# Output projection of an attention layer as seven block products over the whole sum, with its rows turned by DMA, in a kernel on one core

## The chip, the cores and the metric

The kernel runs on one core of a Trainium2 chip. A core has five engines that work side by side, each with its own queue of instructions: TensorE (PE; its weight loads are listed as PEld), VectorE (DVE), ScalarE (ACT), GpSimd (POOL) and SyncE (SP), from whose queue most transfers (DMA) are issued. The metric is the device time of one execution in microseconds, as a median over runs.

## The reference, cut to what matters

An input x of 8 batches, 512 rows, 256 columns goes through four blocks, each added to x after a layer normalization: a linear attention with normalized keys and queries, a feed-forward block (here "f"), a softmax attention with 16 heads of 64, and the same feed-forward block again (here "g").

```python
concat = ctx.reshape(ctx.shape[0], ctx.shape[1], H * P)   # 16 heads x 64 = 1024
out = concat @ l_w.T + l_b                                # 1024 -> 256
...
x = x + _L0_attn_b_ref(_layernorm(x, axis=-1), ...)
x = x + _L0_ffn_ref(_layernorm(x, axis=-1), ...)
```

The change concerns `concat @ l_w.T + l_b`, of 512 x 1024 by 1024 x 256 in each batch. All data are float32; a matmul on float32 shows as two instructions in the profile.

## The kernel before, in words

**Stages.** The heads are worked in pairs, 8 pairs per batch and 64 in all. A loop takes two pairs at a time (32 rounds). In a round, `attend` issues a fixed sequence of score matmuls (line 1081), the maximum (DVE, 1086), exponents (ACT, 1097) and context matmuls (1134); it lasts 13.8 us on PE. It leaves a 128x512 context tile (`ctx`, pool `cpool`) for each pair. Between two such sequences lies a stretch in which PE does everything else: the front of a coming batch (normalizations, linear attention, feed-forward f), projections of queries and keys for the next two pairs (`project_pairs`), of values (`values_fast`), the output projection (`project_out`, label `y`), and the tail of an earlier batch (normalization, feed-forward g, storing).

**Products in blocks.** `project_pairs`, `values_fast` and `keys` already use a scheme of seven block products in place of eight (`seven`): sums of weight blocks are made once, differences of row blocks on POOL for each batch (lines 825 and 573), and seven products are added up in PSUM and by ACT and DVE as they leave it (lines 869, 879, 889, 925, 933). The output projection does not: `project_out` computes rows of x by `rows` (line 429), half of the pairs at a time, with the context as the loaded weights and the output weights `al` as moving data; DVE adds each result from PSUM into x (line 1017).

**Turning rows.** A normalized tile must be transposed. `normed_t` does this on PE; `normed_dma` splits the float32 values into 16-bit parts on POOL (line 408), turns them by a DMA transpose on SP's queue (413), and joins the parts on POOL (417).

**Order.** The order of the instructions on each engine is worked out when the program is built. Every piece of work is a generator that yields its next step: engine, estimated time, time at which its inputs are ready. `Order` keeps an own clock for each engine and picks the step that can start first; among those that start within 0.4 us the one with the lowest rank. A piece has a due period (a pair number) by which it must be done, and a lead, by which its rank falls below that. `until` runs what is due, `fill` adds what fits in a share of PE time. `CHOICES` has for each round a change of the share, a slack and a number that perturbs the ranks. Engines take their instructions in the order so written; real waits go by semaphores. `take` picks one of five PSUM places for a product.

**Buffers.** `buffers(True)` is a set of tiles `xn`, `xr`, `xk`, used by the front of batch 1 and then by the tails of batches 0 to 6; `buffers(False)` serves the other fronts and batch 7's tail. The output bias `lb` is added to x on POOL after each front (line 770).

## Time and profile before

| | us |
|---|---|
| median of 3 runs | 1145.85 (1145.68 to 1146.25) |
| span of the profiled execution, first to last instruction | 1144.2 |
| PE busy | 1124.5 |
| DVE busy | 795.8 |
| ACT busy | 675.1 |
| POOL busy | 461.2 |
| output projection on PE, 512 instructions, summed latencies | 116.1 |

The profile comes from one execution; its own time is given by its span, and the medians of the runs lie 1.65 us above that. Busy times are sums over the instructions of an engine. A matmul's listed time is its latency; matmuls overlap, so that the distance between two starts is what one costs. "PE idle" is time in which no matmul is under way.

### The profile page before, as it was taken

To read this page: it belongs to the slowest core of one execution; us is meant where nothing else is said; L and a number is where in the kernel's file an instruction comes from. 1 tells how busy PE (TensorE), PEld (TensorE's weight loads), DVE (VectorE), ACT (ScalarE), POOL (GpSimd) and SP (SyncE) were. 2 spreads that over 40 slices of the span, in tenths; PEclk is the share of its full clock that TensorE was granted. 3 is DMA by queue.
4 is the path that set the end of the run, shared out by engine and by line. 5 is a ranking of instruction groups with operands and counts; after the bars stand their busy time and mean duration, and the time that the engine had idled before them with its cause. 6 is when DMAs were issued, how large, how long until landed. Compare 5 with 4: busy or idle time off the path is not lost.

```text
span 1144.2 us, 19158 instructions
## 1 busy us (share of the span) xinstructions
PE 1124.5 (98%) x7006; PEld 701.7 (61%) x7006; DVE 795.8 (70%) x1444; ACT 675.1 (59%) x1777; POOL 461.2 (40%) x736
## 2 busy tenths in 40 slices
PE   7999999999999999999999999999999999999998
PEld 4655466655656666666567657666565666666556
DVE  5776767776777676777856767677776776766664
ACT  3546765476564664657645675457765467454653
POOL 4456333352432363344732546353362534421311
PEclk9999999999999999999999999999999999999999
DMA  8000000010001010011010211101101010000001
GB/s 298 1 1 1 10 10 10 11 28 11 1 11 46 19 20 19 1 46 29 19 19 1 56 20 19 19 20 46 19 11 28 19 20 19 10 19 2 19 1 38
DMA packets 61181, 28.63 MB, mean 25 GB/s; under 512 B 51456, under 2 KB 59648, under 8 KB 60576
## 3 DMA queue, kind: packets, MB, share of 16 engines
q1 hardware_dynamic: 59936, 25.70, 9.3%
q8 instruction: 56, 0.92, 0.3%
q10 hardware_dynamic: 864, 1.05, 0.3%
q0 software_dynamic: 288, 0.67, 0.2%
q14 instruction: 37, 0.30, 0.1%
HBM read 10.63 MB, written 4.19 MB: 13 GB/s over the span
## 4 chain that ended last, share of the span: by engine, by line
PE 49%; DVE 1%; POOL 1%; issue 1%; ACT 0%; POOLq 0%; DVEq 0%
PE cx L1134 10%; PE sc L1081 10%; PE m_qk L917 9%; PE y L429 6%; PE m_v L953 4%; PE kv L661 2%; PE r_g L429 2%; PE o_g L429 1%; PE m_k_g L580 1%; PE r_f L429 1%; PE o_f L429 1%; PE k_f L540 1%; PE q L429 1%; DVE xkFalse L733 0%; PE k_g L540 0%
## 5 line engine op out<-in xcount | busy, mean ns | idle before, releaser
L1097 ACT ACTIVATE e<-sc,nm 128x512 f32<-128x512 f32 x512 | 346.7, 689 | 130.0 <-DVE nm L1086 129.8
L1086 DVE TENSOR_REDUCE nm<-sc 128x2 f32<-128x1024 f32 x256 | 308.7, 1218 | 72.1 <-PE sc L1081 71.3
L1081 PE MATMUL sc<-qk 64*64 64x512 f32 x2048 | 263.8, 593 | 3.1 <-DVE qk L889 3.0
L1134 PE MATMUL cx<-e,vs 64*64 64x512 f32 x2048 | 262.3, 589 | 1.0 <-DVE v L974 0.6
L1114 POOL TENSOR_TENSOR vs<-v,rs 128x256 f32<-128x256 f32 x128 | 78.8, 616 | 376.2 <-DVE rs L1110 368.2
L1134 PEld LDWEIGHTS cx<-e,vs 64*64 64x64 f32 x2048 | 85.0, 133 | 136.9 <-issue 114.7
L1081 PEld LDWEIGHTS sc<-qk 64*64 64x64 f32 x2048 | 74.4, 132 | 137.7 <-issue 87.4
L429 PE MATMUL y<-al,ctx 128*128 128x256 f32 x512 | 116.1, 380 | 0.0
L429 PEld LDWEIGHTS y<-al,ctx 128*128 128x128 f32 x512 | 96.7, 190 | 16.3 <-ACT e L1097 2.4
L1097 ACT ACTIVATION_READ_ACCUMULATOR e<-sc,nm 128x1 f32 x512 | 105.4, 206 | 0.0
L925 ACT ACTIVATE qk<-m_qk,bias 128x256 f32<-128x256 f32 x124 | 52.1, 475 | 76.2 <-PE m_qk L917 76.0
L1142 DVE TENSOR_TENSOR ctx<-cx,ctx 128x512 f32<-128x512 f32 x64 | 44.3, 691 | 47.3 <-ACT ctx L1141 47.3
L933 DVE SCALAR_TENSOR_TENSOR qk<-m_qk,dbias,qk 128x256 f32<-128x256 f32 x124 | 54.2, 479 | 20.1 <-PE m_qk L917 19.3
L1017 DVE TENSOR_TENSOR x<-y,x 128x512 f32<-128x512 f32 x32 | 22.1, 689 | 47.7 <-PE y L429 47.7
L661 PE MATMUL kv<-wkv,xrFalse 128*128 128x512 f32 x112 | 52.5, 605 | 0.2 <-DVE st_n L357 0.2
L417 POOL COPY xrFalse<-xkFalse 128x1024 uint16<-128x1024 uint16 x22 | 29.1, 1336 | 44.1 <-DMA xkFalse<-xrFalse 44.1
L1141 ACT COPY ctx<-cx 128x512 f32<-128x512 f32 x64 | 37.4, 584 | 10.8 <-PE cx L1134 10.8
L408 POOL COPY xrFalse<-xnFalse 128x512 uint16<-128x512 uint16 x68 | 39.4, 611 | 6.6 <-ACT xnFalse L381 6.6
L917 PE MATMUL m_qk<-xta,aq 128*128 128x256 f32 x124 | 38.7, 393 | 0.0
L607 POOL TENSOR_TENSOR x<-x,xkFalse 128x512 f32<-128x512 f32 x24 | 30.7, 1283 | 18.0 <-DVE xkFalse L558 7.9
L917 PE MATMUL m_qk<-xta,sums_q 128*128 128x256 f32 x124 | 37.8, 387 | 0.1
L917 PE MATMUL m_qk<-xts,aq 128*128 128x256 f32 x124 | 37.6, 385 | 0.0
(259 smaller groups left out, 1908.6 us busy)
## 6 DMA issues: line engine op xcount, KB each, us to landing
out<-x SPq DMA_DIRECT2D x16, 256.0 KB, 2.1
x<-in_x SPq DMA_DIRECT2D x6, 512.0 KB, 4.3
aq<-in_aq SPq DMA_DIRECT2D x1, 1024.0 KB, 7.8
ak<-in_ak SPq DMA_DIRECT2D x1, 1024.0 KB, 9.9
av<-in_av SPq DMA_DIRECT2D x1, 1024.0 KB, 11.9
al<-in_al SPq DMA_DIRECT2D x1, 1024.0 KB, 14.3
xkFalse<-xrFalse SPq DMA_TRANSPOSE x34, 3.1
x<-in_x ACTq DMA_DIRECT2D x4, 128.0 KB, 4.0
```

The source lines that it names most:

```text
L429: nc.tensor.matmul(ps[:, u * D : (u + 1) * D], lhsT=lhs[i][:, u * P : (u + 1) * P], rhs=rhs[i], start=(i == 0), stop=(i == n - 1),)
L661: nc.tensor.matmul(ps, lhsT=xt[:, kc, u * P : (u + 1) * P], rhs=wkv[:, kc, :], start=(kc == 0), stop=(kc == KC - 1),)
L917: nc.tensor.matmul(ps[:, w * HS : (w + 1) * HS], lhsT=lhs[w][n - 1], rhs=block_of_rows(b, n), start=start and w == 0, stop=True, skip_grou ...
L925: nc.scalar.activation(dst[:, w, :], ps[:, w, :], AF.Identity, bias=bias[:, w, p : p + 1])
L933: nc.vector.scalar_tensor_tensor(dst[:, w, :], ps[:, w, :], dbias[:, w, p // 2 : p // 2 + 1], part[:, w, :], ALU.add, ALU.add,)
L953: nc.tensor.matmul(ps[:, u * HS : (u + 1) * HS], lhsT=block_of_rows(b, n)[:, u * P : (u + 1) * P], rhs=rhs[n - 1], start=start and u == 0, ...
L1081: nc.tensor.matmul(ps[m * HD : (m + 1) * HD, j, :], lhsT=kt[hs, keys], rhs=qt[hs, :], start=True, stop=True,)
L1086: nc.vector.tensor_reduce(nm, ps, AX.X, ALU.max, negate=True)
L1097: nc.scalar.activation(e[:, j, :], ps[:, j, :], AF.Exp, bias=nm[:, j : j + 1], accum_out=sums[g, h][:, c % 2, j : j + 1],)
L1114: nc.gpsimd.tensor_tensor(vs, vh[b, p // 4][:, 2 * h : 2 * h + 2, cols].rearrange("p t (j d) -> p t j d", j=2), rs.unsqueeze(3).to_broadca ...
L1134: nc.tensor.matmul(cx[m][j * HD : (j + 1) * HD, :], lhsT=vsc[g, c // 2][ks, c % 2, j, :], rhs=es[g, c][ks, j, :], start=(c == 0), stop=(c ...
L1142: nc.vector.tensor_tensor(ct, cx[1], ct, ALU.add)
```

## The change: what it does

For batches 0 to 6 the output projection is written in the scheme of seven products. The output is split in two halves of columns and two halves of rows, the sum of 1024 in even and odd pairs (four groups of two pairs). Each product adds all four groups in PSUM, so that it covers the whole sum. The weights `al` are now the loaded operand and the context the moving one, so the result comes out transposed. Sums of weights are made once on POOL (`sums_of_output`), one of them in place of a quarter of `al`, which is loaded again at batch 6. `differences` makes twelve differences of context blocks on POOL, `last_differences` four more. The bias `lc` enters as the results leave PSUM on ACT, the difference of its halves, `dlc`, on DVE. `rows_of_output` turns the result back by two POOL copies, a DMA transpose and a POOL cast per half, and DVE adds it into x. Batch 7 keeps the old form and the old addition of `lb`.

`project_out_fast` of a batch is added in the round of the first two pairs of the next batch (`p == 1`), due in that same period; before, the two halves of the pairs were due at two different periods. It works in `buffers(True)` and waits for the tail of the batch before.

Besides: due periods and leads come from a table, the front is split in three pieces with their own due periods, `CHOICES` is new, some entries moving single pieces in rank, `take` prefers the lowest place and not the highest, three pools have other numbers of buffers, batch 2's first normalization is turned by DMA, and the last batch's second normalization takes the form with two POOL operations and the scaling on DVE. (`CHOICES` and the small helpers `copy`, `add` and `shifted`, which are one instruction each, are left out below.)

```diff
+PLAN = {
+    "linear 0": (-1, 8), "linear 1": (-3, 8), "linear": (-9, 8),
+    "queries 0": (-1, 8), "queries 1": (-3, 8), "queries": (-9, 8),
+    "mean 0": (-1, 8), "mean 1": (-3, 8), "mean": (-9, 8),
+    "front 0": (-1, 8), "front 1": (-3, 8), "front": (-3, 8),
+    "ffn 0": (-1, 8), "ffn 1": (-3, 8), "ffn": (-3, 8),
+    "norm 0": (-1, 8), "norm 1": (-3, 8), "norm": (-3, 8),
+    "rows": (-1, 8), "tail": (15, 0), "keys": (15, 0), "tail last": (17, 16), "tail 6": (17, 0), "keys 6": (17, 0), "pairs": (0, 8),
+    "values 1": (2, 8), "values 0": (4, 8), "y": (0, 8), "y differences": (0, 8),
+    "y rows": (4, 8), "y plain": (2, 0), "y last": (11, 16), "scale": (0, 128),
+    "v 0": (-1, 0), "v 1": (3, 0), "project": (-1, 0), "sums": (0, 0), "late sums": (5, 0),
+}
...
-    def __init__(self, gen, due, lead, number):
-        self.gen, self.due, self.rank, self.number = gen, due, due - lead, number
+    def __init__(self, gen, kind, at, number):
+        due, lead = PLAN[kind]
+        self.gen, self.kind, self.base, self.number = gen, kind, at, number
+        self.due = at + due
+        self.rank = self.due - lead
         self.advance(None)
...
-        a = [(max(t, at), -i) for i, t in enumerate(self.banks) if unheld(t)]
+        a = [(max(t, at), i) for i, t in enumerate(self.banks) if unheld(t)]
...
-    small = ctx.enter_context(tc.tile_pool(name="small", bufs=8))
-    epool = ctx.enter_context(tc.tile_pool(name="epool", bufs=6))
-    cpool = ctx.enter_context(tc.tile_pool(name="cpool", bufs=8))
+    small = ctx.enter_context(tc.tile_pool(name="small", bufs=7))
+    epool = ctx.enter_context(tc.tile_pool(name="epool", bufs=5))
+    cpool = ctx.enter_context(tc.tile_pool(name="cpool", bufs=9))
...
+        nc.gpsimd.dma_start(out=lc, in_=a["lb"].rearrange("(k p) -> p k", p=P))
...
-        ps, ready = yield from normed_t(xb, name, s, h, ready, early=name in ("f0", "f1"))
+        ps, ready = yield from normed_t(xb, name, s, h, ready, early=name in ("f0", "f1", f"g{B - 1}"))
...
-        if b < 3:
+        if b < 2:
...
-        yield "G", 1.3, ready
-        xh = xb[:, 2 * h : 2 * h + 2, :]
-        nc.gpsimd.tensor_tensor(xh, xh, lb.to_broadcast([P, 2, D]), ALU.add)
+        if b == B - 1:
+            yield "G", 1.3, ready
+            xh = xb[:, 2 * h : 2 * h + 2, :]
+            nc.gpsimd.tensor_tensor(xh, xh, lb.to_broadcast([P, 2, D]), ALU.add)
...
+    def output_blocks():
+
+        s = blocks["sums_y"]
+        v = al.rearrange("p (g i) d -> p g i d", i=2)
+        a11, a21, a12, a22 = (v[:, :, i, j * P : (j + 1) * P] for i in range(2) for j in range(2))
+        s1, s2, s4 = (s[:, i, :].rearrange("p (g c) -> p g c", c=P) for i in range(3))
+        return a11, a12, s4, a22, s1, s2, a21
+
+    def sums_of_output():
+
+        a11, a12, s4, a22, s1, s2, a21 = output_blocks()
+        for dst, x0, x1, op in (
+            (s1, a21, a22, ALU.add), (s2, s1, a11, ALU.subtract), (s4, a12, s2, ALU.subtract),
+            (a21, a11, a21, ALU.subtract),
+        ):
+            ready = yield "G", 1.3, 0.0
+            nc.gpsimd.tensor_tensor(dst, x0, x1, op)
+        order.marks["sums_y"] = ready
+
+    def differences(b, ready):
+
+        yield "G", 0.0, ready, -1, ("y", b, "room")
+        s = buffers(True)
+        t3, t2 = (s[n].rearrange("p h (g s) -> p (h g) s", g=2) for n in ("xr", "xk"))
+        for i in range(3):
+            for g in range(NP // 2):
+                (b11, b12), (b21, b22) = halves_of_context(b, g)
+                ready = yield "G", 0.6, ready
+                dst, x0, x1 = (
+                    (t3[:, g, :], b22, b12), (b12, b12, b11), (t2[:, g, :], b22, b12),
+                )[i]
+                nc.gpsimd.tensor_tensor(dst, x0, x1, ALU.subtract)
+            order.marks["y", b, i] = ready
+
+    def last_differences(b, ready):
+
+        t2 = buffers(True)["xk"].rearrange("p h (g s) -> p (h g) s", g=2)
+        for g in range(NP // 2):
+            b21 = halves_of_context(b, g)[1][0]
+            ready = yield "G", 0.6, ready
+            nc.gpsimd.tensor_tensor(b21, b21, t2[:, g, :], ALU.subtract)
+        order.marks["y", b, 3] = ready
+
+    def halves_of_context(b, g):
+
+        return [[ctxt[b, 2 * g + i][:, j * HS : (j + 1) * HS] for j in range(2)] for i in range(2)]
+
+    def project_out_fast(b):
+
+        for h in range(2):
+            if b:
+                yield "G", 0.0, 0.0, -1, ("g", b - 1, h)
+        order.marks["y", b, "room"] = 0.0
+        order.add(differences(b, 0.0), "y differences", NP * b + 9)
+        s = buffers(True)
+        lhs = output_blocks()
+        t3, t2 = (s[n].rearrange("p h (g s) -> p (h g) s", g=2) for n in ("xr", "xk"))
+        rhs = []
+        for g in range(NP // 2):
+            (b11, b12), (b21, b22) = halves_of_context(b, g)
+            rhs.append([b11, b21, b22, b21, b12, t2[:, g, :], t3[:, g, :]])
+        c = [[chunks(s["xn"], j)[:, i, :] for j in range(2)] for i in range(2)]
+
+        def product(n, mark, ps=None):
+            ready = yield "T", 2 * FAST, 0.0, -1, mark, ps is None
+            i = None
+            if ps is None:
+                i = order.take()
+                ps = psum_tile(i, f"m{n}_y_{b}")
+                ps = (ps[:, 0, :] if i < PAIRS else ps)[:, :HS]
+                first = True
+            else:
+                first = False
+            for g in range(NP // 2):
+                nc.tensor.matmul(
+                    ps, lhsT=lhs[n - 1][:, g, :], rhs=rhs[g][n - 1],
+                    start=first and g == 0, stop=True, skip_group_check=True,
+                )
+            return i, ps, ready
+
...
+        i1, ps1, p1 = yield from product(1, "sums_y")
+        u1 = yield from copy(c[0][0], ps1, p1)
+        i6, ps6, p6 = yield from product(6, ("y", b, 2))
+        u2 = yield from add(c[1][0], ps6, c[0][0], max(u1, p6))
+        order.give(i6)
+        i7, ps7, p7 = yield from product(7, ("y", b, 0))
+        u3 = yield from shifted(c[1][1], ps7, c[1][0], max(u2, p7))
+        _, _, p2 = yield from product(2, None, ps1)
+        order.add(last_differences(b, p2), "y differences", NP * b + 9)
+        c11 = yield from copy(c[0][0], ps1, max(p2, u2))
+        order.give(i1)
+        i5, ps5, p5 = yield from product(5, ("y", b, 1))
+        c22 = yield from add(c[1][1], ps5, c[1][1], max(p5, u3))
+        _, _, p3 = yield from product(3, None, ps5)
+        c12 = yield from add(c[0][1], ps5, c[1][0], max(p3, u2))
+        order.give(i5)
+        order.add(rows_of_output(b, 1, max(c12, c22)), "y rows", NP * b + 9)
+        _, _, p4 = yield from product(4, ("y", b, 3), ps7)
+        c21 = yield from shifted(c[1][0], ps7, c[1][0], max(p4, c12))
+        order.give(i7)
+        if b == B - 2:
+            nc.sync.dma_start(
+                out=al.rearrange("p (g i) d -> p g i d", i=2)[:, :, 0, P:],
+                in_=a["al"].rearrange("p (g i) d -> p g i d", i=2)[:, :, 0, P:],
+            )
+        order.add(rows_of_output(b, 0, max(c11, c21)), "y rows", NP * b + 9)
+
+    def rows_of_output(b, h, ready):
+
+        s = buffers(True)
+        apart, turned, y = (s[n].bitcast(U16)[:, h, :] for n in ("xr", "xk", "xn"))
+        columns = y.rearrange("p (k r) -> p k r", k=KC)
+        for k in range(KC):
+            ready = yield "G", 0.6, ready
+            nc.gpsimd.tensor_copy(
+                apart.rearrange("p (l u k d) -> p l u k d", l=2, k=KC, u=2)[:, :, :, k, :],
+                columns[:, k, :].rearrange("p (u d l) -> p l u d", l=2, u=2),
+            )
+        ready = yield "S", 0.9, ready
+        nc.sync.dma_start_transpose(
+            out=turned.rearrange("p (g r) -> p g r", r=P), in_=apart
+        )
+        ready = yield "G", 1.25, ready
+        nc.gpsimd.tensor_copy(
+            y.rearrange("p (u d l) -> p l u d", l=2, u=2),
+            turned.rearrange("p (l u d) -> p l u d", l=2, u=2),
+        )
+        ready = yield "V", 0.62, ready
+        xt = half_of(x[b], h)
+        nc.vector.tensor_tensor(xt, s["xn"][:, h, :], xt, ALU.add)
+        order.add(tail(b, h, ready), "tail 6" if b == B - 2 else "tail", NP * b)
+
...
+    order.add(sums_of_output(), "late sums")
...
+    total -= 7 * 2 * FAST
...
-        if p == 5:
-            order.add(project_out(b, 0), g + 2)
+        if p == 5 and b == B - 1:
+            order.add(project_out(b, 0), "y plain", g)
+        if p == 1 and b > 0:
+            order.add(project_out_fast(b - 1), "y", g)
```

## The prediction

> **What bounds the kernel now.** I read the head of the profile page first, then its chain of waits, then TensorE's (PE's) own waits, then the rows of the operations that the change touches, then the stretches in which the new work must fit.
>
> ```profile
> span 1144.2 us, 19158 instructions
> PE 1124.5 (98%) x7006; PEld 701.7 (61%) x7006; DVE 795.8 (70%) x1444; ACT 675.1 (59%) x1777; POOL 461.2 (40%) x736
> ...
> PE 49%; DVE 1%; POOL 1%; issue 1%; ACT 0%; POOLq 0%; DVEq 0%
> ```
>
> PE is busy 98% of the span, and the chain that ended last is nearly all PE (the shares sum to about half of the span because some matmul records are missing). The next engine stands at 70%. Twenty microseconds are without a matmul, and the stretches say where:
>
> ```profile
> 0.00:30.00 30.00, 22.50 (x74) 13.36 (x74) 16.35 (x47) 12.23 (x39) 14.36 (x35) 1.00 0.79 285
> ...
> 900.00:1050.00 150.00, 149.97 (x993) 95.07 (x995) 107.48 (x182) 84.34 (x216) 52.25 (x78) 1.00 0.07 17
> ...
> 1140.00:1144.20 4.20, 0.00 (x0) 0.00 (x0) 1.10 (x2) 0.00 (x0) 0.00 (x0) 0.97 0.18 62
> ```
>
> The columns are length, then busy time of PE, weight load, DVE, ACT and POOL, then the granted clock. The head loses 7.5 us and the last 4.2 us have no matmul; in the middle PE idles 0.03 us in 150. Adding the loss at each of 32 changes between the 64-wide and the 128-wide matmuls (rows of 8 and 4 that take 1.02 and 1.06 us where the same take 0.86) gives 0.36 x 32 = 11.5 us, which stays whatever the order. So time goes away one for one with PE work, and an order alone has perhaps 5 us to win in the middle.
>
> **What the skill says.** "SBUF — State Buffer", section "Who interferes with whom": a DVE instruction with two SBUF inputs contends with a POOL instruction that reads SBUF, and the second one to issue waits. The trace agrees: the DVE operation of line 733 has a median of 478 ns and a longest of 1493. "PSUM — Partial Sum Buffer", section "Engine vs sequencer instructions": ACT, DVE and POOL queues are strict FIFO, and matmuls start in program order. No matmul in this trace starts ahead of an earlier one, so a product that waits for POOL holds back all PE work behind it. "GPSIMD Engine Reference", section "Elementwise — side-by-side cycle accounting", has POOL about twice as slow as DVE for two inputs; the trace has 1.27 us against 0.69 us for 128x512.
>
> **The change part by part.** These rows carry the prices:
>
> ```profile
> L429 PE MATMUL y<-al,ctx 128*128 128x256 f32 x512 | 116.1, 380 | 0.0
> L1017 DVE TENSOR_TENSOR x<-y,x 128x512 f32<-128x512 f32 x32 | 22.1, 689 | 47.7 <-PE y L429 47.7
> L825 POOL TENSOR_TENSOR xts<-xta x16: 722/727/1252, 93.8 to 979.0; 128x256 f32<-128x256 f32 x16
> L408 POOL COPY xrFalse<-xnFalse 128x512 uint16<-128x512 uint16 x68 | 39.4, 611 | 6.6 <-ACT xnFalse L381 6.6
> L417 POOL COPY xrTrue<-xkTrue 128x1024 uint16<-128x1024 uint16 x14 | 18.5, 1336 | 5.8 <-DMA xkTrue<-xrTrue 5.8
> L770 POOL TENSOR_TENSOR x<-x,lb 128x512 f32<-128x512 f32 x16 | 20.2, 1270 | 1.2 <-ACT xnFalse L381 1.2
> xkTrue<-xrTrue SPq DMA_TRANSPOSE x14, 3.1
> ```
>
> A matmul's row shows its latency (380 ns), not its cost: the chain has "y L429 x16" in 3.45 us, 0.2157 us each from start to start.
>
> 1. *PE, products.* A batch's output projection is 512/8 = 64 instructions, 13.80 us. The new form has seven products of four pair sums in two passes, 7 x 4 x 2 = 56 instructions of the same 128x128 by 256 form, 12.08 us. Weight loads keep their 190 ns below 216 ns and stay hidden. Seven batches: 7 x 8 x 0.2157 = **12.08 us less** on the path.
>
> 2. *PE, transposes.* Batch 2's first normalization goes over to the DMA transpose: 8 PE transposes of 0.109 us (four take 0.43 in the timeline), **0.87 us less**. In return: four POOL copies and two casts (4 x 0.61 + 2 x 1.34 = 5.1 us) and two DMA transposes of 3.1 us; two ACT copies go (1.2 us). POOL is 48% busy between 60 and 150 us, and the new due time is 6 pair steps ahead of need, so I cost it at nothing; uncovered it is one latency of some 8 us, once.
>
> 3. *POOL.* Gone: 14 of 16 bias additions, 14 x 1.27 = 17.8 us. Added per batch: 12 + 4 differences of 128x256, 16 x 0.727 = 11.6 us, and for two halves two copies and a cast each, 2 x (2 x 0.61 + 1.34) = 5.1 us; seven batches 117 us. Once: four sums of weights, 4 x 1.27 = 5.1 us. Batch 2's 5.1 as above. POOL goes from 461 to about 571 us, half the span: hidden as a total. It is not hidden where a product waits for it (below).
>
> 4. *DVE and ACT.* Gone: 28 additions x 0.69 = 19.3 us. Added per batch: three additions of 0.42 and two shifted joins of 0.48 from PSUM, and two additions of 0.69 into x, 3.6 us, 25 in all. DVE gains 6 us of 796, ACT two copies of 0.475 per batch, 6.7 us of 675. Both have 30% or more free: nothing.
>
> 5. *SP's queue.* 16 more transposes. They stand among output stores and other transposes and each holds SP until its copies are done. SP already waits 325.8 us ahead of output stores with no harm to PE. The reload of a quarter of the weights (256 KB) at batch 6 also waits on SP, for the last product. The nearest loads, 256 KB, land in 3 to 6 us, and the plain products of batch 7 come two periods (some 60 us) later: nothing. A late load would cost those few microseconds, once.
>
> 6. *Small.* One more short bias load from POOL's queue at about 21 us (0.55 us of POOL) in the head, 0 to 0.6 us. The shift it feeds sits beside the DVE step at 63.6 us, 35 us after landing at the neighbours' 6 us. One fewer exponent buffer: in the second half of an attention step the exponents then wait for the context matmuls issued just ahead of them. Those end 0.86 us after the scores; the maximum that the exponents wait for anyway takes 1.22 us. Covered by 0.36 us; the tenth context tile is likewise needed only after the products, which are due before it. The last batch's earlier normalization has two POOL operations fewer (0.22 + 0.20) and DVE in place of ACT (2 x 0.41 against 1.1 us): 0.5 us gained at an end where PE has gaps of 0.36 and 0.16 us; I take 0.3.
>
> 7. *The new order and its waits.* A product waits for twelve differences: 12 x 0.727 = 8.7 us, while the planner counts 0.6 each, 7.2 us. They can start about 1.7 us into the stretch between two attention steps, after the two scalings of values that end there (511.49 and 512.60 in the timeline, 509.84 being the stretch's start). So product six is ready about 10.5 us in. Ahead of it can go product one (1.73 us), the seven steps of the next pair (28 x 0.2157 = 6.04 us), and the value products (6.04 us): 13.8 us, enough by 3.3. Behind product six wait all other PE work and then the attention step. If the planner puts product six just at its own ready time, PE loses 1.5 us in that batch. The last product waits four differences, 2.9 us, under two products of 1.73: covered. A product added into a bank that DVE has just read waits 0.42 + about 0.2 us if nothing lies between. From zero to about 2.1 us a batch, 0 to 15 in all; the work at hand speaks for the lower part. I take 0.25 us x 7 = 1.75 us. A new order may also win back up to about 3 of the 5 us; I count none.
>
> The sum on the profile's span: 1144.2 - 12.08 - 0.87 - 0.3 + 1.75 = 1132.7 us. The median stands 1.65 us above the span, so **1134.3 us**.
>
> **Rivals.** (a) *Partial stalls.* Product six and the last product come late by 0.7 to 1.5 us in most batches, as the planner's 0.6 us suggests; 5 to 10 us return, 1137.5 to 1142.5. For it:
>
> ```profile
> 747.74:771.21 23.47, 23.41 (x103) 18.37 (x105) 17.79 (x36) 11.50 (x32) 15.47 (x25) 1.00 0.07 23
> 886.10:909.44 23.34, 23.31 (x98) 17.68 (x100) 16.35 (x36) 10.05 (x31) 12.50 (x20) 1.00 0.04 12
> ```
>
> These are two of the seven stretches in which the new products stand. POOL is busy 12.5 and 15.5 of 23.4 us already; 11.6 more makes 24 to 27. Against it: the due times move other POOL work away, and fourteen bias additions go. (b) *POOL becomes the bound of these stretches, slower than before.* The differences queue behind 5 to 6 us of other POOL work, and PE stands at product six. The change is even at 13.25 - 7k = 0, k = 1.9 us per batch, and slower by 0.2% from 2.2 us. With k = 3 us (product six ready near 14 us, 11 us of work ahead of it), 21 us return: 1145.85 - 13.25 + 21 = 1153.6 us. Against it: PE is in-order but its order is written with POOL's load counted. (c) *The order wins too.* PE's middle losses shrink by 3 us or more: 1129.5 us and below. (d) *The gain is hidden*, because PE was not the limit: within 0.2% of 1145.85. The 149.97 of 150 us speaks against it.
>
> **How the numbers follow.** Covered, 1131 to 1137: 0.58, and the forecast is 1134.3. (a) 0.24, of which 0.02 lies within 0.2%. (b) 0.08. (c) 0.08. (d) 0.02. 0.2% (2.3 us) is about what a measurement can tell from no change. Faster 0.58 + 0.22 + 0.08 = 0.88, same 0.04, slower 0.08. The range takes in the covered case, (a) nearly whole, and the nearer part of (c): 1129 to 1142 us. The likeliest case's own range is 1131 to 1137.
>
> **What would show it.** After: the y matmuls fall to 7 x 56 + 64 = 456; PE busy falls by about 13 us to near 1111; POOL near 570. A wait row of PE or its weight loads on POOL for the y products shows step 7, and its total says which case holds: below 3 us covered, 5 to 10 (a), over 15 (b). DVE rows of two SBUF inputs grow in mean if the shared port bites. The forecast is wrong if the stretches after the first attention step of each batch show PE idle by more than 1 us, if the attention steps grow longer than 13.8 us for want of buffers, or if the end after the last context matmul, 28.8 us now, grows because batch 6's tail comes late (at most about 5 us).

## The result, and the profile after

| | before | after |
|---|---|---|
| median, us | 1146.04 (11 runs, 1145.68 to 1147.15) | 1143.57 (11 runs, 1142.37 to 1144.73) |
| span of the profiled execution, us | 1144.2 | 1142.3 |

The ratio is 0.9976, with a 95% interval of 0.9967 to 0.9985. The change makes the kernel about 2.5 us faster. The forecast was 11.6 us, and 1143.57 lies outside its range, 1129 to 1142. One execution of a later kernel (new products with the old settings) took 2452 us, its 256-wide matmuls 0.443 us apart where 0.216 is usual; no ratio below uses it.

The head of the page after, and the shares of the chain of waits:

```profile
span 1142.3 us, 19417 instructions
PE 1116.8 (98%) x6942; PEld 698.6 (61%) x6942; DVE 805.7 (71%) x1470; ACT 676.4 (59%) x1785; POOL 568.8 (50%) x883
...
PE 88%; DVE 6%; ACT 3%; issue 1%; POOL 1%; DMA 1%; DVEq 0%; POOLq 0%; ACTq 0%
```

PE has 64 matmuls fewer, as worked out (7 x 8 of products and 8 of transposes). Its busy time falls by only 7.7 us. A matmul's listed time is its latency, and of the time that is lost below about half lies under a listed matmul. POOL is at the 571 us of the prediction. The chain's shares can't be set beside those of before as they stand: the chain before is followed back only to 547.6 us, so its shares cover half of the span (missing matmul records, which the prediction gave as the reason, were not shown to be it). From about 548 us to the end, some 595 us in both, DVE holds 13.8 us of the chain before and 26.6 after, ACT 2.3 and 12.2. So time that passes through these two engines has come onto the path.

The same stretches as before, columns as in the prediction:

```profile
0.00:30.00 30.00, 22.52 (x71) 12.56 (x71) 15.18 (x45) 12.09 (x39) 14.07 (x35) 1.00 0.80 284
...
450.00:600.00 150.00, 147.74 (x925) 94.81 (x928) 108.28 (x193) 88.82 (x237) 81.32 (x126) 1.00 0.14 27
...
900.00:1050.00 150.00, 149.29 (x981) 95.48 (x983) 101.68 (x173) 83.63 (x215) 71.55 (x105) 1.00 0.12 24
```

The head is unchanged. In the middle PE is without a matmul for 0.71 us of the 150 from 900 us on, where it was 0.03. Over the five such windows from 300 to 1050 us it is 7.4 us (150 less each PE time, 147.74 the lowest), and was 1.6 before.

Groups of instructions that the change added, and one (line 753) that it did not touch:

```profile
L1129 PE MATMUL m_y<-ctx,al 128*128 128x256 f32 x168 | 39.7, 379 | 0.0
...
L753 DVE SCALAR_TENSOR_TENSOR xkFalse<-xkFalse,rnq,gf 128x256 f32<-128x256 f32 x28 | 23.3, 876 | 3.4 <-ACT gf L741 3.3
...
L1095 POOL TENSOR_TENSOR ctx<-ctx,xkTrue 128x256 f32<-128x256 f32 x28 | 19.5, 728 | 8.0 <-PE m_y L1129 8.0
```

The last number of the first row says that PE was never idle ahead of these products, and the three other forms of the new products have the same 0.0. So the wait that steps 7, (a) and (b) of the prediction turned on does not exist. The second row is a scaling in a batch's front that is the same instruction as before. There it had a mean of 704 ns (line 733); now it has 876.

Two waits of PE are new. These rows give the wait, its total in us, how often it came and its longest; the kernel before has neither:

```profile
PE m_qk L949 <- DVE qk L965: 4.5, 7, 0.7
PE sc L1258 <- ACT e L1274: 3.8, 6, 1.1
```

**Where the 12.95 us of PE work went.** The distances between the starts of consecutive matmuls, summed once over the attention steps (64-wide matmuls) and once over the stretches between them, close the account. Work is the number of matmuls times the undisturbed distance of their form; what is left of a stretch is idle.

| us | before | after | change |
|---|---|---|---|
| ahead of the first matmul | 6.55 | 6.34 | -0.2 |
| PE work in the stretches | 658.41 | 645.46 | -12.95 |
| idle in the stretches | 25.9 | 30.0 | +4.1 |
| attention steps | 448.59 | 455.28 | +6.7 |
| after the last matmul | 4.8 | 5.2 | +0.4 |

The saving is there to the hundredth (12.08 + 0.87). 10.8 us of it is given back in two places, neither of which is a wait of the new products.

**First place: the attention steps.** A step takes 13.9 us in both kernels as a rule. Before, four steps took longer, by 2.6 us together. After the change twelve do, by 9.7 us: the five behind the fourth stretches by 6.8, one other by 1.2 (13.9 us when the changed kernel was run again), and six behind third stretches by 1.7. In nearly every batch the stretches between the steps follow one pattern, from batch 1 on with 24.2, 16.4, 7.8 and 31.0 us of PE work. The steps behind the fourth stretch take 15.14, 15.65, 14.95, 15.65 and 14.95 us, the one other 15.10, and the steps behind the third stretch 14.1 to 14.3. This is the timeline at the start of such a step, all engines, many lines left out (start, duration, then engine and line; PE's scores begin at 456.17):

```profile
454.89 1.26 POOL L627 TENSOR_TENSOR x<-x,xrTrue 128x512 f32<-128x512 f32 x1 [0.37 <-DVE xrTrue L578]
455.01 1.81 DVE L753 SCALAR_TENSOR_TENSOR xkFalse<-xkFalse,rnq,gf 128x256 f32<-128x256 f32 x2 [0.20 <-ACT gf L741]
456.17 1.09 PE L1258 MATMUL sc<-qk 64*64 64x512 f32 x8
...
456.75 0.68 DVE L578 SCALAR_TENSOR_TENSOR xrTrue<-xrTrue,o_g 128x512 f32<-128x512 f32 x1
456.97 1.27 POOL L627 TENSOR_TENSOR x<-x,xkFalse 128x512 f32<-128x512 f32 x1 [0.82 <-DVE xkFalse L753]
...
457.35 2.59 DVE L753 SCALAR_TENSOR_TENSOR xkFalse<-xkFalse,rnq,gf 128x256 f32<-128x256 f32 x2
...
458.20 1.46 POOL L627 TENSOR_TENSOR x<-x,xrTrue 128x512 f32<-128x512 f32 x1
...
459.86 3.47 DVE L1263 TENSOR_REDUCE nm<-sc 128x2 f32<-128x1024 f32 x3
...
462.61 0.66 PE L1258 MATMUL sc<-qk 64*64 64x512 f32 x4 [1.05 <-ACT e L1274]
```

The first scores are done near 457.3, and the maximum on them (1263) usually starts 1.16 us after the scores began. Here it starts after 3.69 us. Ahead of it in DVE's queue stand four scalings of line 753 and an addition (578). Beside POOL's additions (627) three of them take 1.18 to 1.49 us, where one takes 0.47 alone. The late maximum makes the exponents late, and PE's fourth group of scores waits for a PSUM place that these exponents free. Over the five steps behind the fourth stretch the first maximum came at +2.98 to +3.69 us, and the step's length was 13.9 us plus what exceeded 1.94: 2.99 gives 14.95, 3.20 gives 15.14, 3.69 gives 15.65. Read from these five, a lateness up to about 0.78 us is absorbed and every microsecond beyond it counts once. It is no rule for every step: in the kernel before, first maxima at +2.04, +2.52 and +2.73 all went with 14.7 us, and the six steps behind the third stretch are long with a first maximum at +1.16.

These scalings are not new work. What is new is their place. Before, in a front of the same kind, they stood well inside a stretch (the next step's scores began at 909.37):

```profile
897.68 2.69 DVE L733 SCALAR_TENSOR_TENSOR xkFalse<-xkFalse,rnq,gf 128x256 f32<-128x256 f32 x4 [0.32 <-ACT gf L721]
...
910.53 1.23 DVE L1086 TENSOR_REDUCE nm<-sc 128x2 f32<-128x1024 f32 x1 [0.21 <-PE sc L1081]
```

In the five fronts from 300 us on all twenty scalings started at least 3.07 us ahead of the next step before the change; after it, eighteen of the twenty start between 1.16 us ahead of a step's scores and 2.28 us behind their start. Beside POOL they took up to 1.49 us before as well, but they had ended when the next step began. So this loss belongs to the new order and not to the work that the change added to DVE.

**Second place: the third stretch.** Its idle time is 1.41 to 1.52 us in six batches and 1.84 in the first, where a stretch loses 0.2 at the least. The timeline of PE inside one:

```profile
546.27 0.59 PE L949 MATMUL m_qk<-xta,sums_k 128*128 128x256 f32 x2
547.58 0.70 PE L949 MATMUL m_qk<-xts,aq 128*128 128x256 f32 x2 [0.71 <-DVE qk L965]
```

A product of the query and key projections waits for DVE to join an earlier one (line 965), and no other PE work stands between. Between 85 and 1100 us stretches of at most 12.1 us of work were three before, with 4.3 us idle in all; now they are eleven, with 15.3. The other stretches fell from 11.6 us (28 of them) to 6.3 (20). So the new order wins 5.3 us in the others, as rival (c) said, and loses 11.0 in thin ones (1.6 of both is only the 0.2 us of eight stretches that changed class). The old product had two halves of 6.9 us of PE work, which needed four finished pairs and nothing else; they could be put into stretches that lacked work. That is where they stood: between 85 and 1100 us nineteen stretches hold some of them, with 6.1 to 19.4 us of other work, 13.0 in the middle one, and eight of the nineteen would have at most 12.1 us without them; the twelve others have 20.3 in the middle. The new product is a single block of 12.1 us that needs all eight pairs, and stands in the first stretch. That the missing halves are what makes the third stretch thin is argued from this; the new due periods, by which the fourth stretch holds 31.0 us, are a rival, and no run separates the two.

### The profile page after: what moved, and what is told of

The parts are those of the page before. It is cut to its first block, busy times and chain, and to the rows that moved or that the text cites. A ratio compares the mean times of both kernels' runs of the same rounds, so it can differ in the third digit from the quotient of the medians.

```text
span 1142.3 us, 19417 instructions
## 1 busy us (share of the span) xinstructions
PE 1116.8 (98%) x6942; PEld 698.6 (61%) x6942; DVE 805.7 (71%) x1470; ACT 676.4 (59%) x1785; POOL 568.8 (50%) x883
## 4 chain that ended last, share of the span: by engine, by line
PE 88%; DVE 6%; ACT 3%; issue 1%; POOL 1%; DMA 1%; DVEq 0%; POOLq 0%; ACTq 0%
PE sc L1258 19%; PE cx L1311 18%; PE m_qk L949 14%; PE m_v L985 8%; PE m_y L1129 7%; PE kv L681 5%; PE r_g L449 2%; PE o_f L449 2%; PE k_f L560 2%; PE r_f L449 2%; PE q L449 2%; PE m_k_g L600 2%; PE o_g L449 2%; ACT e L1274 2%; DVE xkFalse L753 1%; PE y L449 1%
## 5 line engine op out<-in xcount | busy, mean ns | idle before, releaser
L1258 PE MATMUL sc<-qk 64*64 64x512 f32 x2048 | 274.0, 595 | 6.9 <-ACT e L1274 3.8
L1311 PE MATMUL cx<-e,vs 64*64 64x512 f32 x2048 | 273.2, 590 | 0.0
L1291 POOL TENSOR_TENSOR vs<-v,rs 128x256 f32<-128x256 f32 x128 | 82.9, 650 | 292.1 <-DVE rs L1287 280.7
L1311 PEld LDWEIGHTS cx<-e,vs 64*64 64x64 f32 x2048 | 92.0, 133 | 131.7 <-issue 104.9
L1258 PEld LDWEIGHTS sc<-qk 64*64 64x64 f32 x2048 | 78.5, 132 | 140.8 <-issue 70.4
L437 POOL COPY xrFalse<-xkFalse 128x1024 uint16<-128x1024 uint16 x24 | 31.8, 1335 | 22.9 <-DMA xkFalse<-xrFalse 22.8
L1129 PE MATMUL m_y<-ctx,al 128*128 128x256 f32 x168 | 39.7, 379 | 0.0
L949 PE MATMUL m_qk<-xta,ak 128*128 128x256 f32 x124 | 36.9, 379 | 0.0
L949 PE MATMUL m_qk<-xta,sums_k 128*128 128x256 f32 x124 | 36.9, 379 | 0.0
L949 PE MATMUL m_qk<-xts,ak 128*128 128x256 f32 x124 | 36.9, 379 | 0.0
## 6 DMA issues: line engine op xcount, KB each, us to landing
av<-in_av SPq DMA_DIRECT2D x1, 1024.0 KB, 12.2
al<-in_al SPq DMA_DIRECT2D x1, 1024.0 KB, 14.3
```

Source lines behind the costliest of these rows:

```text
L949: nc.tensor.matmul(ps[:, w * HS : (w + 1) * HS], lhsT=lhs[w][n - 1], rhs=block_of_rows(b, n), start=start and w == 0, stop=True, skip_grou ...
L1129: nc.tensor.matmul(ps, lhsT=lhs[n - 1][:, g, :], rhs=rhs[g][n - 1], start=first and g == 0, stop=True, skip_group_check=True,)
L1258: nc.tensor.matmul(ps[m * HD : (m + 1) * HD, j, :], lhsT=kt[hs, keys], rhs=qt[hs, :], start=True, stop=True,)
L1291: nc.gpsimd.tensor_tensor(vs, vh[b, p // 4][:, 2 * h : 2 * h + 2, cols].rearrange("p t (j d) -> p t j d", j=2), rs.unsqueeze(3).to_broadca ...
L1311: nc.tensor.matmul(cx[m][j * HD : (j + 1) * HD, :], lhsT=vsc[g, c // 2][ks, c % 2, j, :], rhs=es[g, c][ks, j, :], start=(c == 0), stop=(c ...
```

## The experiments

All ratios are to the kernel before, run on the same chip with them. Where nothing else is said, the edit is one to the changed kernel. "Theory A" of the expectations is the account above in its first form: the loss comes from where work stands in the order. Its rivals are told in each.

**An eighth of the old products left out, in the old order** (on the kernel before).

```diff
-                    stop=(i == n - 1),
+                    stop=(i == n - 1 - (left_out and u == 1)),
                 )
+                if left_out and u == 1 and i == n - 2:
+                    break
...
+                left_out=b < B - 1,
```

> The kernel before in its own order, but for batches 0 to 6 one in eight matmuls of the output projection is left out (the sums lack those terms): 12.08 us less PE work, no new product, no new wait. Theory A and rival B: nearly the whole 12 us, 1133.5 to 1136. Rival C: 1139 us or more, the rest coming back as waits for ACT and DVE.

1133.7 us, 0.9894 (0.9878 to 0.9911); span 1131.5, attention steps 448.1. For 12.08 us of PE work less the kernel is 12.7 us faster. PE time was worth its face value, as step 1 says, so long as everything else stays in place. The gain is not hidden by another bound: rival (d) falls, and the question is what the new form brought with it.

**New products with the old settings of the order** (before's list `CHOICES`, its scale of the perturbation, its preference of PSUM places and its due periods for the fronts).

```diff
...
-    "linear 0": (-1, 8), "linear 1": (-3, 8), "linear": (-9, 8),
+    "linear 0": (-1, 8), "linear 1": (-3, 8), "linear": (-3, 8),
...
-        a = [(max(t, at), i) for i, t in enumerate(self.banks) if unheld(t)]
+        a = [(max(t, at), -i) for i, t in enumerate(self.banks) if unheld(t)]
...
-        return ((h >> 8) % 1000 / 1000 - 0.5) * (24, 12, 6)[v % 3] + moved
+        return ((h >> 8) % 1000 / 1000 - 0.5) * 24 + moved
```

> The new products with the order settings of before (rank perturbations and shares of before, fronts due as before, highest free bank first, batch 2 still turned by DMA). Theory A (placement: the new projection can only stand in the first stretch of a batch, and the old halves, which had filled the thin stretches, are gone, so work piles up in some stretches whatever the settings): no better than the changed kernel, 1140 to 1152 us. Rival B (the new settings alone cost the missing 11 us): 1133 to 1137 us. Rival C (PE time isn't worth its face value, since less PE work only bares ACT and DVE): 1140 us or more, as A.

1280.03 us, 1.1166 (1.1148 to 1.1185). A further execution of the same kernel was taken for its profile:

> The kernel of new products with the settings of before once more, for a profile of an execution at the usual matmul rate (in the first profile every matmul took about twice as long, 0.46 us where 0.216 is usual). Theory A: its 1280 us come from a few places where PE stands at a wait of 5 us or more, and stretches as uneven as 1 us and 31 us. Rival C: the loss is spread evenly over all stretches and attention steps.

1274.07 us, span 1272.0. PE's waits in it:

```profile
PE k_f L558 <- ACT prev_f L524: 15.6, 2, 13.2
PE k_f L558 <- DVE prev_f L467: 12.4, 1, 12.4
```

PE's work in the stretches is 645.46 us, the changed kernel's own. Their idle time is 122 us instead of 30.0 and the attention steps take 492.2. The stretches are between 1 and 40 us long. The two largest waits, 28.0 us together, are PE standing before a feed-forward product whose input is not yet mixed, far from the new products. The rest of the 122 us is spread over many smaller ones.

**Old products with the new settings** (all eight batches in the old form, with the old addition of `lb` and without the sums of output weights).

```diff
...
-        if p == 5 and b == B - 1:
+        if p == 5:
...
-        if p == 1 and b > 0:
-            order.add(project_out_fast(b - 1), "y", g)
```

> All eight batches with the old projection and its halves due as before, everything else (due periods, choices, banks, pools) as in the changed kernel. Theory A: the thin stretches are filled again, the idle time in the stretches between attention steps falls back to about 26 us; if the late first maxima come from the new due periods of the fronts, the attention steps still sum to 453 us or more and the time is 1150 to 1153; if they come with the new products, 449 us and 1145 to 1148. Rival B: 1143.6 + 12 = 1155 to 1158 us.

1215.59 us, 1.0607 (1.0591 to 1.0622); attention steps 484.5, idle in the stretches 60. This too loses far more than either explanation gave it. The two runs together say that a list of choices serves only the set of work that it was chosen for: crossing it with the other set costs 70 to 135 us. They do not say which part of the settings is to blame, and they cannot be used to split the 2.5 us into a part of the products and a part of the order. Two things can be read from the second one's trace. Seven stretches between 85 and 1100 us have at most 12.1 us of work although the halves are there, so the new settings can make thin stretches by themselves. And in four of its five fronts from 300 us on the scalings of line 753 stand 7.3 us or more ahead of the next step, so the new settings alone do not fix their place.

**No differences on POOL.** The sixteen subtractions per batch are not issued, so no new product waits for them; PE has the same matmuls.

```diff
-                nc.gpsimd.tensor_tensor(dst, x0, x1, ALU.subtract)
...
-            nc.gpsimd.tensor_tensor(b21, b21, t2[:, g, :], ALU.subtract)
...
-            rhs.append([b11, b21, b22, b21, b12, t2[:, g, :], t3[:, g, :]])
+            rhs.append([b11, b22, b22, b11, b11, b22, b22])
```

> The changed kernel in its own order without the sixteen differences per batch: POOL does not issue them (81 us of POOL work less) and the seven products read context blocks that no difference writes, so no product waits for POOL (sums are wrong for that; PE work is the same). Theory A (the waits of the new products are covered): within 2 us of the changed kernel. The rivals on record, in which products stand at PE's head waiting for POOL's differences: 5 to 15 us less, 1129 to 1138.

1144.27 us, 0.9982 (0.9975 to 0.9988), against 0.9978 (0.9969 to 0.9986) for the changed kernel itself, run again beside it:

> The changed kernel itself, beside the next two on the same chip: 0.997 to 0.999 of the kernel before, as measured.

1143.96 us. POOL's busy time falls from 568.8 to 492.7 us, and attention steps (455.3) and stretches (675.7) stay. The 76 us of differences cost nothing. Step 7's term of 1.75 us and rivals (a) and (b) have no ground.

**POOL's addition beside the scaling left out** (the sum of linear attention and x, from batch 2 on).

```diff
-        ready = yield from add_to(xb, h, s["r"][:, h, :], ready, adder(b))
+        if b < 2:
+            ready = yield from add_to(xb, h, s["r"][:, h, :], ready, adder(b))
+        else:
+            ready = yield "G", 1.3, ready
```

> The changed kernel in its own order, but for batches 2 to 7 POOL's addition of the linear attention into x is not issued (the planner still counts it; the output lacks that term). Theory A with its second part (DVE's scaling at the start of a batch's first attention step is held by POOL's additions, so that the first maximum comes 3.0 to 3.7 us after the first scores and not 1.2, and the step lasts 15.0 to 15.7 us and not 13.9): the five long steps shrink by 0.7 us or more each and the time falls by 3 to 6 us, to 1138 to 1141. If POOL's additions are not what holds DVE: within 1 us of the changed kernel.

1140.07 us, 0.9946 (0.9931 to 0.9961). Attention steps 450.78 us (-4.5), stretches 676.3 (+0.8). Three of the five steps behind the fourth stretch are back to 13.9 us and the two others fall from 15.65 to 14.95, as expected. PE's order and work are unchanged, so the lengthening of these five did come from DVE and POOL.

**The scaling moved off DVE** (from batch 2 on: ACT multiplies by the row factor, POOL by the column factor).

```diff
-            nc.vector.scalar_tensor_tensor(
-                qs[:, u, :], qs[:, u, :], rn[:, u : u + 1], gf, ALU.mult, ALU.mult
+            if b < 2:
+                nc.vector.scalar_tensor_tensor(
+                    qs[:, u, :], qs[:, u, :], rn[:, u : u + 1], gf, ALU.mult, ALU.mult
+                )
+            else:
+                nc.scalar.activation(qs[:, u, :], qs[:, u, :], AF.Identity, scale=rn[:, u : u + 1])
+        if b >= 2:
+            nc.gpsimd.tensor_tensor(
+                qs, qs, gf.unsqueeze(1).to_broadcast([P, 2, D]), ALU.mult
+            )
```

> The changed kernel with its PE order untouched and a right result: for batches 2 to 7 the scaling of the linear attention is taken off DVE, ACT multiplies by the row's factor and POOL by the column's, then POOL adds as before. Theory A: DVE is free at the start of a batch's first attention step, the first maximum comes 1.2 to 1.6 us after the first scores, the five long steps go back to 13.9 to 14.2 us, and the time falls by 4 to 7 us, to 1137 to 1140. If POOL's extra 2.5 us then delays its scaled values: half of that.

1140.24 us, 0.9944 (0.9927 to 0.996): faster than both kernels, and the best version that this study has. The same place in its timeline (its scores begin at 459.03):

```profile
459.03 1.09 PE L1265 MATMUL sc<-qk 64*64 64x512 f32 x8
459.14 0.69 DVE L578 SCALAR_TENSOR_TENSOR xrTrue<-xrTrue,o_g 128x512 f32<-128x512 f32 x1 [1.47 <-PE o_g L449]
...
460.19 1.22 DVE L1270 TENSOR_REDUCE nm<-sc 128x2 f32<-128x1024 f32 x1 [0.36 <-PE sc L1265]
```

The maximum starts 1.16 us after the scores, as in an undisturbed step, and four of the five steps concerned take 13.90 us. The first of its kind, at 317 us, does not gain (15.65, in the changed kernel 15.14): there DVE stands 3.96 us at statistics that wait for POOL's addition, and the maximum behind them starts at +3.69. Attention steps sum to 449.94 us (-5.3), the stretches to 676.82 (+1.4, 1.2 of it in one new wait of a value product). POOL's busy time rises by 14.6 us and ACT's by 11.1 with no harm seen apart from that step: what counted was not the load of an engine but what stood ahead of one instruction.

**A second DVE step moved as well** (on top of the last one: for half of the rows the mix of the first column, line 471, goes to ACT in two instructions).

```diff
-            first_column(ps, name, h, i)
+            if h == 0:
+                first_column(ps, name, h, i)
+            else:
+                for kc in range(KC):
+                    nc.scalar.activation(
+                        ps[:, kc, 0:1], edge[name][:, kc, :], AF.Identity, scale=omu[:, i, kc : kc + 1]
+                    )
```

> The kernel with the scaling off DVE, and besides DVE's product of two small tiles for the first column of a half (128x2, 0.16 us when free, 0.70 to 1.26 us where POOL works beside it) given to ACT in two instructions. PE order untouched, result right. Theory A (a DVE instruction with two SBUF inputs stands still while POOL works, and what is behind it on DVE is late): the attention steps of 14.15 and 15.1 us go back to 13.9, 1.5 to 3 us less than with the scaling alone, 1137 to 1139. If these were late for another reason: as with the scaling alone, 1140.

1141.74 us, 0.996 (0.9945 to 0.9975), attention steps 451.54: a miss. The six steps behind third stretches went from 14.15 to 13.90 us as expected. But three steps behind the second stretch now take 15.16 us. One of them starts at 665.77:

```profile
665.92 1.34 POOL L437 COPY xrTrue<-xkTrue 128x1024 uint16<-128x1024 uint16 x1
...
667.30 0.19 ACT L520 COPY edge_g<-xrTrue 128x2 f32<-128x2 f32 x1 [0.98 <-POOL xrTrue L437]
...
668.17 0.87 DVE L538 SCALAR_TENSOR_TENSOR xkTrue<-xrTrue,mu,prev_g 128x256 f32<-128x256 f32 x2 [1.53 <-ACT prev_g L534]
...
668.96 3.48 DVE L1276 TENSOR_REDUCE nm<-sc 128x2 f32<-128x1024 f32 x3
```

DVE now stands 1.53 us at a mix that waits for ACT, which waits for POOL's cast, and the maximum again starts 3.19 us after the scores. No DVE instruction is slowed by POOL here. So the cause is wider than a conflict of two engines: a wait that holds DVE's queue ahead of the first maximum lengthens the step as well.

**Three microseconds moved into the third stretch.** Each new product leaves out one of its four matmuls, and as many are repeated in the projections of the third stretch: seven matmuls of two instructions each, 14 x 0.2157 = 3.02 us per batch.

```diff
+            if p == NP - 2 and b < B - 1:
+                nc.tensor.matmul(
+                    ps[:, HS:], lhsT=lhs[1][n - 1], rhs=block_of_rows(b, n),
+                    start=False, stop=True, skip_group_check=True,
+                )
...
-            for g in range(NP // 2):
+            for g in range(NP // 2 - 1):
```

> The changed kernel, its order untouched, with 3.02 us of PE work per batch moved: each of the seven new products leaves out one of its four matmuls in the first stretch, and in the third, thin stretch of batches 0 to 6 each of the seven query and key products repeats one matmul (sums are wrong for that; PE work is the same in sum, 7 x 3.02 us moved). Theory A: in the thin stretches the idle time falls from 1.4 to 1.5 us to about 0.4, so the time falls by 5 to 8 us, to 1136 to 1139. If thin stretches cost nothing: 1143 to 1144.

1141.47 us, 0.9955 (0.994 to 0.997), not the 1136 to 1139 that were expected. PE's work is the same. The third stretch loses its idle time (from 1.52 to 0.21 us wherever it was filled) and the 14.14 us step behind it its excess. The stretches together are 6.4 us shorter, but the attention steps 3.3 us longer: behind the shortened first stretch they take 14.63 to 15.78 us where they took 13.9. The thin stretch is thus a loss of its own, and the filler has to come from somewhere where it is not cover itself. Here half of the gain came back as the first effect in another place.

**The tail due earlier** (due period 13 and lead 8 for the tail and its keys, not 15 and 0), which was to even the stretches out.

```diff
-    "rows": (-1, 8), "tail": (15, 0), "keys": (15, 0), "tail last": (17, 16), "tail 6": (17, 0), "keys 6": (17, 0), "pairs": (0, 8),
+    "rows": (-1, 8), "tail": (13, 8), "keys": (13, 8), "tail last": (17, 16), "tail 6": (17, 0), "keys 6": (17, 0), "pairs": (0, 8),
```

> The changed kernel with the tail of a batch and its block products due one stretch earlier and with the lead of the other work (13 and 8 in place of 15 and 0): PE work in the four stretches of a batch becomes about 24, 16, 21 and 17 us in place of 24, 16, 8 and 31. Theory A: with even stretches the thin ones no longer idle, and the end of the fourth no longer crowds DVE and POOL: 1132 to 1139. Against it: the tail's chain through POOL and DMA may not be ready one stretch earlier; PE then waits several us in each batch, 1145 to 1165.

1213.74 us, 1.0588 (1.0573 to 1.0604), worse than either expectation. Attention steps 457.6, idle in the stretches 96.5. The stretches got more even in part: 24, 16, 21 and 15 us of work in one batch, but 24, 6, 26 and 23 in another. More work in the third stretch is by itself no cure:

```profile
PE r_g L449 <- DVE xrTrue L532: 16.4, 7, 3.7
...
PE o_g L449 <- ACT xnTrue L618: 6.9, 4, 2.0
```

The tail's feed-forward block stands in PE's queue before its input has come through POOL, the DMA transpose and DVE; these two rows are 23.3 of the 96.5 us, and the other waits are smaller ones. Work is filler only if it is ready where it is put.

## Why the prediction was wrong, point by point

- **What bounds the kernel.** Right in kind: 12.08 us of PE work are worth 12.7 us with all else unchanged. What was read too widely is the 149.97 of 150 us, the best of five such windows. It shows that PE had work at hand in that order, not that another order would have it too.
- **Steps 1 and 2, PE.** Exact: 12.08 + 0.87 us, and 12.95 us of work gone in the trace.
- **Step 3, POOL.** Total right (571, measured 568.8), and hidden as said.
- **Step 4, DVE and ACT: this step failed.** The added work was right (+6 us on DVE, measured +10, of which 28 x 0.172 = 4.8 us is line 753 growing from 704 to 876 ns). The conclusion from it, "both have 30% or more free: nothing", judged a place by an average. DVE is free on average and occupied for up to 3.7 us just where five attention steps need it, which makes these 6.8 us too long; with the smaller changes of the others the attention steps take +6.7 us, the larger part of the miss. What holds DVE there is old work in a new place, so the same loss stands against step 7. The prediction quoted the price itself, the longest 1493 ns of line 733 beside a median of 478, and "SBUF — State Buffer" of the Trainium skill, section "Who interferes with whom", as its cause; the trace after agrees (1.49 us for the last scaling beside POOL's addition). It did not ask what stands behind that instruction.
- **Step 5, SP's queue.** Nothing was lost there: no wait row of PE names a transfer.
- **Step 6, small terms.** The exponents' missing buffer does not show: in the run with the scaling moved, the steps with an early first maximum take 13.90 us apart from those behind the third stretch, and these too take 13.90 in the run with the second DVE step moved. So the attention steps did grow, one of the prediction's signs of being wrong, but not for want of buffers. The end after the last context matmul grew from 28.9 to 32.4 us, which the prediction named as a sign against it. But 3.45 us more PE work stands there (26.32 against 22.87), and idle time in it fell from 1.20 to 0.83 us. Nothing came late.
- **Step 7, the new order: this step failed too.** Its term, the waits of the products for the differences, was 1.75 us and measured nothing. For the order itself it counted "none" without a reason: it did not look at how much PE work each stretch would hold, nor at what would stand on DVE when a step begins. In the stretches the order gave +4.1 us: +11.0 in thin ones, -5.3 in the others, the rest at the two ends. With the +6.7 us of the attention steps the new order cost 10.8 us where the prediction had none. How much of this belongs to the new products and how much to the new settings is not known.
- **The rivals.** (a) has a time close to the measured one, 1137.5 to 1142.5, and a mechanism that was not there. (b) and (d) fell. (c) was true for 5.3 us and was outweighed.
- **The sum mended.** 1144.2 - 12.95 + 6.7 + 4.1 - 0.2 + 0.4 = 1142.3 us, the span measured.

**What stays open.** The run with the scaling moved recovers 3.9 us of the span, and the move of three microseconds 3.3. A kernel with both was not run, and if the two added up, 3.6 us of the 10.8 would still have no version that recovers them. Why the order is so easily lost, by 70 us for another due period and lead of the tail, was not settled; the waits name late inputs of the tail and the fronts, not the choice behind them. The longer steps behind the third stretch were made short by freeing DVE of a 128x2 step, but whether by that step's own time or by the place of the next one was not separated.

## What to carry to other kernels

A microsecond taken from the busiest engine was worth a microsecond here only while the order around it stayed: ask what the removed instructions may have been covering, and look at how much work each stretch will hold afterwards. For a stage that is paced by a chain of engines, look at what stands ahead of its first link in that engine's queue when the stage begins; an engine with 30% free on average can be late there every time. Settings of an order that were picked for one set of work are part of that set.

## What the hardware did that was not expected

In the run with the tail due earlier, PE stands still for 3.7 us and then runs slowly. PE's timeline:

```profile
870.32 3.62 PE L449 MATMUL o_f<-fv,xnFalse 128*128 128x256 f32 x16
877.65 3.65 PE L449 MATMUL r_g<-fr,xrTrue 128*128 128x256 f32 x8 [3.72 <-DVE xrTrue L532]
883.91 3.21 PE L449 MATMUL r_g<-fr,xrTrue 128*128 128x256 f32 x8 [2.61 <-DVE xrTrue L532]
```

Sixteen matmuls take 3.62 us ahead of the pause, and eight of the same form take 3.65 behind it; the granted clock is 0.53 over these eight and 0.59 over the next. "TensorE: Matmul & The Clock Gate" of the Trainium skill, section "What's actually happening", has the clock halved after an idle window of about 3.4 us, which agrees; the second pause, of 2.61 us only, is followed by slow matmuls as well. By the distances of starts in the stretches behind the kernel's head about 44 matmuls of that run are slow and cost 9.5 us in all, 45 and 9.6 us in the one with new products and old settings, 17 and 3.7 us in the one with old products and new settings, none in the changed kernel. So a lost order pays for its long waits a second time.

The smallest DVE instruction is not small beside POOL: the mix of the first column (line 471, 128x2, two inputs in SBUF) has a median of 161 ns in one of its groups. In the other the median is 496 ns and the longest 1258, at a moment when one of POOL's additions of 1.26 us runs.
